# A fused time-attention, band-attention and feed-forward kernel: runs of eight steps, transposed copies on ACT, output products behind the scores, residual sums a run ahead

## The chip, the cores and the metric

The kernel runs on one core of one Trainium2 chip. The metric is device time in microseconds (us) of one execution. The kernel before took 3129.98 us, the median of 3 runs (3129.38 to 3130.77). Its profiled execution took 3130.63 us.

Names of the engines are those of the profile: PE (matrix products, with PEld for its weight loads), DVE (vector), ACT (scalar functions), POOL (GpSimd), SP (which issues the DMAs).

## The reference, cut to what matters

The input `x` has the shape 2 x 256 x 128 x 128 (batch, time T, band FB, channel C), all in float32. Three layers with residual sums follow one another; each head has 32 channels and there are 4 heads.

```python
xt = _ln(x, ...).transpose(0, 2, 1, 3)
x = x + _mha(xt, t_wi, t_bi, t_wo, t_bo, H_T, cm).transpose(0, 2, 1, 3)   # over time, causal mask
xf = _ln(x, ...)
x = x + _mha(xf, f_wi, f_bi, f_wo, f_bo, H_F, bm)                        # over bands, |i - j| <= 16
xn = _ln(x, ...)
h = jax.nn.gelu(xn @ w1.T + b1, approximate=False)                       # 128 -> 512 -> 128
x = x + (h @ w2.T + b2)
```

`_ln` subtracts the mean over the channels and multiplies with the inverse root of the variance. `_mha` is the usual attention: products for queries, keys and values, scores, softmax, weighted values, output product.

## The kernel before, in words

A short start-up folds the norms' weights into the product weights and tests whether the scores are bounded. They are for these inputs, so the program takes `bounded_path`, where softmax needs no maximum. (`shifted_path` is the other branch and does not run.)

The work is cut into **groups** of 512 tokens. There are three kinds, all classes with the same method names:

- `OverTime`: 128 groups, each two bands times 256 time steps. All of them come first, and write their result to DRAM (`x1`).
- `OverBands`: 128 groups, each 4 time steps times 128 bands, read from `x1`; they leave their result in SBUF, in a tile `x2` of 16 time steps.
- `FeedForward`: 128 groups, each on a quarter of an `x2` tile; they write the output.

In the second half of the program four `OverBands` groups and the four `FeedForward` groups on the same tokens take turns: 32 **cycles** of 4 + 4. Because gelu on one side and exponential and logarithm on the other are in different function tables of ACT, ACT loads a table at each turn.

The methods of a group, with the tiles by which the trace names them, are these. `load` starts the DMA of `xt` or `xb`. `statistics` makes mean and variance (`stats`, `mv`, on DVE) and in the same method the inverse root (`rstd`, on POOL). `normalize` makes `xh` (DVE, four instructions). `transpose` makes `xp` (PE, four transposes), and `take_transposed` copies it to SBUF as `xnT` (DVE). `queries_keys` and `values` are the products `qp`, `kp`, `vp`; they are copied to `qT` (ACT), `kT` (DVE for time groups, ACT for band groups) and `v` (ACT). The scores `sp` are products over 32 channels of one head, so four heads lie beside one another in four strips of 32 rows of PE. ACT takes the exponential (`pt` or `pf`), and POOL then cuts the mask out with selects; of the four heads of a band group, POOL does three with two selects each, and DVE the last by a product with a 0/1 tile `band`. `weigh` makes the row sums `rp` and the weighted values `op`; their weights are 32 columns wide, so four heads lie in four strips of columns. `invert` takes `ln` and `exp(-ln)` of the row sums on ACT (`ln`, `r`), and `divide` makes `oT` from it with three DVE instructions (`t`, `u`, `oT`). `divide_alone` does it with a DVE reciprocal instead, at one place per cycle. `output` is the output product `yp`, and `finish` adds it to the residual sum (`rd` or `x`), which `bias` prepared on POOL. A feed-forward group has four products `hp` with gelu (`hT`), sixteen small products `zp`, and its residual sum `res`.

The time groups split scores and exponential into two halves (`first_half`, `second_half`), feed-forward groups do so with their products; a band group does all in the first half.

The order of the work is written out by hand, by `run`: one pass of its loop is one **step** n. In a step, parts of several groups are interleaved: scores and exponential of group n, weighted values and division of group n - 1, the output product of group n - 2, the products for queries, keys and values of group n + 1, the transposes of group n + 2, the statistics of group n + 3. Each engine is wrapped in `InOrder`, which pins its instructions to the order of emission; all those instructions therefore carry one line number in the profile (L798, and L812 in the changed kernel). So an engine never passes a waiting instruction. DMAs are issued by SP, in order as well.

All PSUM tiles come from one pool of 8 banks, taken in turn. `xpool` has 3 buffers for `xt`/`xb` and, with a tag of its own, 2 for `x2`. The pool `work` has 3 buffers of most tiles, 2 of `t`, `u`, `oT`, `ln`, `r`, and 5 of `rd`.

Of the kernel before, what the change touches and what calls it, by code (L numbers as in the profile page):

```python
# [26 lines left out]
GB = 16  # L27
SAFE = 30.0
# [395 lines left out]
class Group:  # L424
# [4 lines left out]

    AHEAD = 2  # L430

# [12 lines left out]
    def statistics(self):  # L444
        path, vector, gpsimd = self.path, self.path.vector, self.path.gpsimd
        self.mv = path.small.tile([P, NT, 2], F32, name="mv")
        stats = path.small.tile([P, NT, 6], F32, name="stats")
        for i in range(NT):
            vector.bn_stats(stats[:, i, :], self.src()[:, i, :])
        for i in range(NT):  # L450
            vector.bn_aggr(self.mv[:, i, :], stats[:, i, :])
        self.rstd = path.small.tile([P, NT], F32, name="rstd")
        gpsimd.tensor_scalar(self.rstd, self.mv[:, :, 1], EPS, None, ALU.add)
        gpsimd.tensor_tensor(self.rstd, self.rstd, path.k.mhalf, ALU.pow)

    def normalize(self):
        path, vector = self.path, self.path.vector
        self.xh = path.work.tile([P, NT, P], F32, name="xh")
# [23 lines left out]

    def second_half(self):
        pass

    def second_function(self):
        pass
# [32 lines left out]
class Attention(Group):  # L520
# [60 lines left out]
    def divide_alone(self):  # L581

        path, vector = self.path, self.path.vector
        r = path.work.tile([P, NT * P], F32, name="r", bufs=2)
        vector.reciprocal(r, self.rp)
        self.oT = path.work.tile([P, NT * P], F32, name="oT", bufs=2)
        vector.scalar_tensor_tensor(self.oT, self.op, -1.0, r, ALU.mult, ALU.mult)

# [18 lines left out]
class OverTime(Attention):  # L607
# [26 lines left out]
    def weights(self, s):  # L634
        path = self.path
        for h in range(H):
            path.scalar.activation(self.p[:, s, h, :], self.sp[h], AF.Exp)
        for n in (0, 2):
# [12 lines left out]

    def second_half(self):
        self.scores(1)

    def second_function(self):
        self.weights(1)

# [23 lines left out]
class OverBands(Attention):  # L681


    which = 1

# [9 lines left out]
    def weights(self, heads):  # L695
        path = self.path
        for h in heads:
            path.scalar.activation(self.p[:, h].rearrange("p i q -> p (i q)"), self.sp[h], AF.Exp)
        for h in heads:
            blk = self.p[:, h]  # L700
            if h == H - 1:
                path.vector.tensor_tensor(blk, blk, path.band.unsqueeze(1).to_broadcast([P, NT, P]), ALU.mult)
                continue
            for s in (1, -1):
                path.gpsimd.affine_select(
                    out=blk, in_=blk, compare_op=ALU.is_ge, fill=path.zero, base=BAND,
                    pattern=[[0, NT], [-s, P]], channel_multiplier=s,
                )

# [8 lines left out]

    def first_function(self):
        self.weights(range(H))  # L720
# [17 lines left out]
class FeedForward(Group):  # L738
    AHEAD = 1
# [63 lines left out]
class BoundedPath:  # L803
# [22 lines left out]
    def groups(self, x, out):  # L826
# [28 lines left out]
        for b in range(B):  # L855
            x1v = k.x1[b].rearrange("t f c -> f t c")
            outv = out[b].rearrange("t f c -> f t c")
            for t0 in range(0, T, GB):
                held = {}

                def load(t0=t0, x1v=x1v, held=held):
                    held["x"] = self.xpool.tile([P, GB, C], F32, name="xb", tag="x")
                    nc.sync.dma_start(held["x"], x1v[:, t0 : t0 + GB, :])
                    held["x2"] = self.xpool.tile([P, GB, C], F32, name="x2", tag="x2", bufs=2)

                def part(name, g, held=held):
                    return lambda: held[name][:, g : g + NT, :]

                for g in range(0, GB, NT):
                    yield OverBands(self, part("x", g), part("x2", g), load if g == 0 else None)  # L870
                for g in range(0, GB, NT):

                    def store(t, g=t0 + g, outv=outv):
                        nc.sync.dma_start(outv[:, g : g + NT, :], t)

                    yield FeedForward(self, part("x2", g), None, None, store)

    def run(self, x, out):
# [7 lines left out]
        def near(n, far, name):  # L886

            for d in (1, 2):
                if 0 <= n + d + far < len(groups) and groups[n + d + far].AHEAD == d:
                    do(n + d + far, name)  # L890

# [3 lines left out]
        def move(n):  # L895
            near(n, 0, "transpose")
            near(n, 0, "take_transposed")

        self.scalar.preload_act_table_set(EXP_SET)
        for n in range(-7, len(groups) + 2):  # L900
            feeding = [at(n - i, FeedForward) for i in range(3)]
            do(n + 7, "load")
            near(n, 0, "normalize")
            if feeding[0] and at(n - 1, OverBands):

                do(n, "first_half", "first_function", "second_half", "second_function")
                do(n - 2, "output", "finish")
                near(n, 1, "statistics")
                move(n)
                do(n, "bias")  # L910
                do(n - 1, "weigh", "divide_alone")
            elif feeding[1] and at(n - 2, OverBands):
                do(n, "first_half", "first_function", "bias")
                do(n - 1, "weigh", "divide")
                move(n)
                do(n - 2, "output", "finish")
                near(n, 1, "statistics")
                do(n, "second_half", "second_function")
            else:
                do(n - 2, "output", "finish")  # L920
                near(n, 1, "statistics")
                if feeding[1] and at(n, OverBands):
                    self.scalar.preload_act_table_set(EXP_SET)
                do(n, "first_half", "first_function", "bias")
                early = at(n, OverBands) and at(n + 1, FeedForward)
                if early:
                    move(n)
                do(n - 1, "weigh", "invert", "divide")
                if feeding[0] and at(n + 1, FeedForward):
                    move(n)  # L930
                    early = True
                do(n, "second_half", "second_function")
                do(n + 1, "queries_keys", "take_query", "take_key", "values", "take_values")
                if not early:
                    move(n)
# [69 lines left out]
```

## Time and profile before

| what | value |
|---|---|
| median of 3 runs | 3129.98 us |
| time of the profiled execution | 3130.63 us |
| its span, first to last instruction | 3128.7 us |
| PE busy (matrix products) | 3013.3 us, 96% |
| PEld busy (weight loads) | 2133.5 us, 68% |
| DVE busy | 2246.7 us, 72% |
| ACT busy | 1748.6 us, 56% |
| POOL busy | 1889.3 us, 60% |
| granted clock of PE | 0.999 |
| ACT table loads | 64 of 1283 ns |
| POOL selects on `pf` | 768 of 711 ns |

The time of the profiled execution is 1.9 us above its span; the work stands in the span. A busy share is a mean over the whole program. In a row of the timeline the first number is the start, the second the time from the first start to the last end of the instructions that the row merges. Ends of products on PE are modelled and the next product usually starts ahead of them, so the price of a product on PE is read from its start to the next start. What stands in brackets is idle time of the engine ahead of that row, and what ended it.

### The profile page before, as it was taken

To read this page: it belongs to the slowest core of one execution; us is meant where nothing else is said; L and a number is where in the kernel's file an instruction comes from. 1 tells how busy PE (TensorE), PEld (TensorE's weight loads), DVE (VectorE), ACT (ScalarE), POOL (GpSimd) and SP (SyncE) were. 2 spreads that over 40 slices of the span, in tenths; PEclk is the share of its full clock that TensorE was granted. 3 is DMA by queue.
4 is the path that set the end of the run, shared out by engine and by line. 5 is a ranking of instruction groups with operands and counts; after the bars stand their busy time and mean duration, and the time that the engine had idled before them with its cause. 6 is when DMAs were issued, how large, how long until landed. Compare 5 with 4: busy or idle time off the path is not lost.

```text
span 3128.7 us, 77496 instructions
## 1 busy us (share of the span) xinstructions
PE 3013.3 (96%) x31270; PEld 2133.5 (68%) x31270; DVE 2246.7 (72%) x6414; ACT 1748.6 (56%) x3200; POOL 1889.3 (60%) x2441
## 2 busy tenths in 40 slices
PE   7999999999999999999999999999999999999998
PEld 5666666666666666666666666666666666776676
DVE  6776767777677677677767767776777677767775
ACT  4666666666666664554455445544554555455544
POOL 4666666666666665566556656665665566556654
PEclk9999999999999999999999999999999999999999
DMA  3222222222222221101111111111101110111000
GB/s 84 59 59 72 59 59 60 71 59 61 72 61 59 59 62 35 35 28 43 34 35 28 45 35 32 28 45 35 32 28 45 35 32 28 45 35 32 28 22 22
DMA packets 222863, 140.55 MB, mean 45 GB/s; under 512 B 7968, under 2 KB 205984, under 8 KB 222496
## 3 DMA queue, kind: packets, MB, share of 16 engines
q1 hardware_dynamic: 221248, 134.45, 15.3%
q8 instruction: 249, 4.08, 0.5%
q10 hardware_dynamic: 1248, 1.05, 0.1%
q14 instruction: 118, 0.97, 0.1%
HBM read 68.36 MB, written 67.11 MB: 43 GB/s over the span
## 4 chain that ended last, share of the span: by engine, by line
PE 80%; DVE 13%; ACT 5%; issue 1%; DMA 0%; POOL 0%; SPq 0%; ACTq 0%; POOLq 0%; DVEq 0%
PE zp L798 15%; PE hp L798 15%; PE sp L798 10%; PE yp L798 7%; PE rp L798 7%; PE qp L798 6%; PE op L798 6%; PE vp L798 5%; PE kp L798 5%; PE xp L798 4%; DVE xh L798 3%; ACT pf L798 3%; DVE stats L798 2%; DVE oT L798 2%; DVE t L798 1%; DVE x L798 1%
## 5 line engine op out<-in xcount | busy, mean ns | idle before, releaser
L798 POOL TENSOR_SCALAR rstd<-mv 128x4 f32<-128x4 f32 x384 | 99.2, 258 | 1131.9 <-DVE mv L798 1131.9
L798 ACT ACTIVATE hT<-hp,b 128x512 f32<-128x512 f32 x512 | 351.9, 687 | 620.8 <-PE hp L798 616.4
L798 ACT ACTIVATE pt<-sp 128x384 f32<-128x384 f32 x1024 | 419.3, 496 | 303.6 <-PE sp L798 303.6
L798 POOL TENSOR_SCALAR_AFFINE_SELECT pf<-pf 128x512 f32<-128x512 f32 x768 | 533.9, 711 | 38.6 <-ACT pf L798 12.3
L798 PEld LDWEIGHTS zp<-w2T_sb,hT 128*128 128x128 f32 x4096 | 475.0, 192 | 50.4 <-issue 38.7
L798 PE MATMUL hp<-xnT,w1f 128*128 128x512 f32 x1024 | 471.5, 598 | 34.0 <-DVE xnT L798 34.0
L798 PE MATMUL zp<-w2T_sb,hT 128*128 128x128 f32 x4096 | 481.5, 276 | 0.1
L798 DVE COPY xnT<-xp 128x512 f32<-128x512 f32 x384 | 260.0, 684 | 278.9 <-PE xp L798 278.9
L798 POOL TENSOR_TENSOR rstd<-rstd,mhalf 128x4 f32<-128x4 f32 x384 | 399.7, 1041 | 32.0
L798 PE MATMUL sp<-qT,kT 32*128 32x128 f32 (+1 forms) x8192 | 389.4, 315 | 0.0
L798 ACT ACTIVATE pf<-sp 128x512 f32<-128x512 f32 x512 | 264.4, 602 | 202.9 <-PE sp L798 202.6
L798 PEld LDWEIGHTS sp<-qT,kT 32*128 32x128 f32 x8192 | 310.8, 185 | 64.6 <-issue 35.9
L798 PEld LDWEIGHTS vp<-wf,xnT 128*128 128x128 f32 x2048 | 269.1, 192 | 123.0 <-issue 85.5
L798 PEld LDWEIGHTS hp<-xnT,w1f 128*128 128x128 f32 x1024 | 181.9, 190 | 218.6 <-issue 162.4
L798 PE MATMUL yp<-wn,oT 128*128 128x128 f32 x2048 | 275.1, 277 | 46.8 <-DVE oT L798 46.8
L798 POOL TENSOR_SCALAR_AFFINE_SELECT pt<-pt 128x512 f32<-128x512 f32 x512 | 314.4, 636 | 0.0
L798 PEld LDWEIGHTS yp<-wn,oT 128*128 128x128 f32 x2048 | 251.1, 192 | 73.9 <-ACT v L798 58.6
L798 PE MATMUL qp<-xnT,wf 128*128 128x512 f32 x512 | 282.7, 634 | 1.2 <-DVE xnT L798 1.2
L798 DVE TENSOR_TENSOR t<-rp,r 128x512 f32<-128x512 f32 x224 | 154.5, 690 | 174.8 <-ACT r L798 173.9
L798 PE MATMUL vp<-wf,xnT 128*128 128x128 f32 x2048 | 269.9, 275 | 0.0
L798 DVE TENSOR_SCALAR xh<-x,mv,rstd 128x128 f32<-128x128 f32 x512 | 256.3, 562 | 15.1 <-POOL rstd L798 15.1
L798 PE MATMUL kp<-xnT,wf 128*128 128x512 f32 x512 | 262.3, 594 | 0.0
(94 smaller groups left out, 4630.5 us busy)
## 6 DMA issues: line engine op xcount, KB each, us to landing
xt<-in_x SPq DMA_DIRECT2D x64, 512.0 KB, 5.5
x<-rd SPq DMA_DIRECT2D x256, 128.0 KB, 1.9
out<-res SPq DMA_DIRECT2D x128, 256.0 KB, 2.3
xb<-x SPq DMA_DIRECT2D x32, 0.5 KB, 6.1
w1T_sb<-in_w1T ACTq DMA_DIRECT2D x1, 256.0 KB, 3.8
w2T_sb<-in_w2T ACTq DMA_DIRECT2D x1, 256.0 KB, 4.2
t_wiT_sb<-in_t_wiT ACTq DMA_DIRECT2D x1, 192.0 KB, 2.5
f_wiT_sb<-in_f_wiT ACTq DMA_DIRECT2D x1, 192.0 KB, 3.9
```

The source lines that it names most:

```text
L798: return self.tc.keep_in_program_order(emit(*args, **kwargs))
```

## The change

What it does:

- **Longer runs.** Band groups and feed-forward groups now take turns in runs of 8 + 8 (`RUN = 32` time steps), 16 runs in place of 32 cycles. There are 4 `x2` buffers in place of 2, and 4 of `xh` in place of 3. Loads are issued 10 steps ahead, not 7.
- **Transposed copies.** `xnT` of band and feed-forward groups is copied by ACT, not DVE. Time groups keep DVE.
- **Output product behind the scores.** In a step, the scores of group n now come first, then the output product of group n - 2. Before it was the other way round.
- **Residual sums a run ahead.** `bias` of a band group (POOL) is made 8 steps ahead: in the feed-forward steps of the run before, or in the last eight time steps.
- **Split methods.** The inverse root leaves `statistics` and becomes `root`, which comes after `normalize`; masks leave the exponential's methods and become `first_mask` and `second_mask`. In the last band group of a run, DVE masks two heads and POOL two.
- **The turn.** All groups are now normalized two steps ahead (feed-forward groups before: one). `divide_alone` with its reciprocal is gone; in the first feed-forward step of a run, the last band group's `invert` stands between the two halves of gelu.

The diff, cut to its core:

```diff
+RUN = 32
...
     def statistics(self):
...
+
+    def root(self):
+        path, gpsimd = self.path, self.path.gpsimd
         self.rstd = path.small.tile([P, NT], F32, name="rstd")
         gpsimd.tensor_scalar(self.rstd, self.mv[:, :, 1], EPS, None, ALU.add)
         gpsimd.tensor_tensor(self.rstd, self.rstd, path.k.mhalf, ALU.pow)
...
-        path.vector.tensor_copy(self.xnT, self.xp)
+        if isinstance(self, OverTime):
+            path.vector.tensor_copy(self.xnT, self.xp)
+        else:
+            path.scalar.copy(self.xnT, self.xp)
...
-    def divide_alone(self):
...
+    def second_mask(self):
+        path = self.path
+        for h in range(H - self.by_vector, H):
+            blk = self.p[:, h]
+            path.vector.tensor_tensor(blk, blk, path.band.unsqueeze(1).to_broadcast([P, NT, P]), ALU.mult)
...
+            for r0 in range(0, T, RUN):
+                run = []
+                for t0 in range(r0, r0 + RUN, GB):
...
+                        held["x2"] = self.xpool.tile([P, GB, C], F32, name="x2", tag="x2", bufs=2 * RUN // GB)
...
+                    if i == len(run) - 1:
+                        g.by_vector = 2
...
-        for n in range(-7, len(groups) + 2):
-            feeding = [at(n - i, FeedForward) for i in range(3)]
-            do(n + 7, "load")
-            near(n, 0, "normalize")
-            if feeding[0] and at(n - 1, OverBands):
-
-                do(n, "first_half", "first_function", "second_half", "second_function")
-                do(n - 2, "output", "finish")
-                near(n, 1, "statistics")
-                move(n)
-                do(n, "bias")
-                do(n - 1, "weigh", "divide_alone")
...
+        for n in range(-10, len(groups) + 2):
+            feeds = [at(n - 2 + i, FeedForward) for i in range(5)]
+            bands = [at(n - 2 + i, OverBands) for i in range(5)]
+            do(n + 10, "load")
+            do(n + 3, "statistics")
+            if bands[2] and feeds[1]:
+                self.scalar.preload_act_table_set(EXP_SET)
+            do(n, "first_half", "first_function", "first_mask")
+            if feeds[1]:
+                if bands[0]:
+                    do(n - 2, "output", "finish")
                 do(n - 1, "weigh", "divide")
+            elif feeds[2]:
+                do(n - 1, "weigh", "invert", "divide")
+            else:
+                do(n - 2, "output", "finish")
+            if feeds[3]:
+                do(n + 1, "transpose", "take_transposed")
+            do(n + 2, "normalize")
+            do(n + 3, "root")
+            if not bands[2]:
+                do(n, "bias")
+                if at(n + RUN // NT, OverBands):
+                    do(n + RUN // NT, "bias")
+            if bands[2]:
+                do(n, "second_mask")
+            if not feeds[1] and not feeds[2]:
                 do(n - 1, "weigh", "invert", "divide")
+            do(n, "second_half", "second_function")
+            if not bands[2]:
+                do(n, "second_mask")
+            if feeds[2] and bands[1]:
+                do(n - 2, "output", "finish")
+            do(n + 1, "queries_keys", "take_query", "take_key", "values", "take_values")
+            if at(n + 2, Attention):
+                do(n + 2, "transpose", "take_transposed")
```

PE in the time stage, one step, before (`yp` belongs to group n - 2, the first two `sp` rows to group n):

```order
L798 MATMUL yp<-wn_106,oT 128x128 x4
L798 MATMUL sp<-qT,kT 128x256 x4
L798 MATMUL sp<-qT,kT 128x128 x4
L798 MATMUL rp<-pt,ones 32x512 x4
L798 MATMUL rp<-pt,ones 32x2x128 x4
L798 MATMUL op<-pt,v 32x256 x4
L798 MATMUL op<-pt,v 32x128 x4
```

And the same place now:

```order
L812 MATMUL sp<-qT,kT 128x256 x4
L812 MATMUL sp<-qT,kT 128x128 x4
L812 MATMUL yp<-wn_106,oT 128x128 x4
L812 MATMUL rp<-pt,ones 32x512 x4
L812 MATMUL rp<-pt,ones 32x2x128 x4
L812 MATMUL op<-pt,v 32x256 x4
L812 MATMUL op<-pt,v 32x128 x4
```

The full-size product `yp` stood ahead of the products in strips; now it stands between the strips of rows (`sp`) and the strips of columns (`rp`, `op`). In band steps the same two pieces change places.

DVE in the band stage, before, from the sum `x` of one step to that of the next (`x_15240` is a tile of residual sums):

```order
L798 TENSOR_TENSOR x_15240<-yp,x_15240 128x512
L798 BN_STATS stats<-x_15240 128x6 x4
L798 BN_AGGR mv<-stats 128x2 x4
L798 TENSOR_TENSOR pf<-pf,band 128x512
L798 TENSOR_TENSOR t<-rp,r_16398 128x512
L798 TENSOR_TENSOR u<-op,r_16398 128x512
L798 SCALAR_TENSOR_TENSOR oT<-t,u 128x512
L798 TENSOR_SCALAR xh<-x_15240,mv,rstd 128x128 x4
L798 TENSOR_TENSOR x_15240<-yp,x_15240 128x512
```

And now:

```order
L812 TENSOR_TENSOR x_14871<-yp,x_14871 128x512
L812 TENSOR_SCALAR xh<-xb,mv,rstd 128x128 x4
L812 TENSOR_TENSOR pf<-pf,band 128x512
L812 TENSOR_TENSOR t<-rp,r_16421 128x512
L812 TENSOR_TENSOR u<-op,r_16421 128x512
L812 SCALAR_TENSOR_TENSOR oT<-t,u 128x512
L812 BN_STATS stats<-xb 128x6 x4
L812 BN_AGGR mv<-stats 128x2 x4
L812 TENSOR_TENSOR x_14871<-yp,x_14871 128x512
```

The normalization `xh` has moved to between the sum `x`, which waits for `yp`, and the `oT` that the next `yp` waits for; the statistics have moved out of there.

ACT at the turn from the last band group of a run to feed-forward, before:

```order
L798 ACTIVATE pf<-sp 128x512 x4
L798 ACTIVATE ln<-rp 128x512
L798 ACTIVATE r_17865<-ln 128x512
L798 ACT_TABLE_LOAD
L798 ACTIVATE hT<-hp,b_181 128x512 x16
```

And now:

```order
L812 ACTIVATE pf<-sp 128x512 x4
L812 COPY xnT<-xp 128x512
L812 ACTIVATE ln<-rp 128x512
L812 ACTIVATE r_19705<-ln 128x512
L812 ACT_TABLE_LOAD
L812 ACTIVATE hT<-hp,b_181 128x512 x2
L812 ACT_TABLE_LOAD
L812 ACTIVATE ln<-rp 128x512
L812 ACT_TABLE_LOAD
L812 ACTIVATE r_19754<-ln 128x512
L812 COPY xnT<-xp 128x512
L812 ACT_TABLE_LOAD
```

Where one table load stood, four stand now (the last is followed by the other gelus), since `ln` and `r` of the last band group have come between the gelus. The program has 80 table loads on this path in place of 64.

More of the change, by code (lines that the diff above doesn't have):

```diff
@@ L457, in normalize @@
         path, vector = self.path, self.path.vector
-        self.xh = path.work.tile([P, NT, P], F32, name="xh")
+        self.xh = path.work.tile([P, NT, P], F32, name="xh", bufs=4)
         for i in range(NT):
@@ L481, in first_function, with first_mask @@
         pass
+    def first_mask(self):
+        pass
     def second_half(self):
@@ L486, in second_function @@
     def second_function(self):
+        pass
+    def second_mask(self):
         pass
@@ L693, in scores, with first_function, first_mask @@
                 path.tensor.matmul(self.sp[h][:, c], self.kT[r, c], self.qT[r, c], start=True, stop=True)
-    def weights(self, heads):
+    def first_function(self):
+        for h in range(H):
+            self.path.scalar.activation(self.p[:, h].rearrange("p i q -> p (i q)"), self.sp[h], AF.Exp)
+    def first_mask(self):
         path = self.path
-        for h in heads:
-            path.scalar.activation(self.p[:, h].rearrange("p i q -> p (i q)"), self.sp[h], AF.Exp)
-        for h in heads:
+        for h in range(H - self.by_vector):
             blk = self.p[:, h]
-            if h == H - 1:
-                path.vector.tensor_tensor(blk, blk, path.band.unsqueeze(1).to_broadcast([P, NT, P]), ALU.mult)
-                continue
             for s in (1, -1):
```

72 lines of the change are left out of this document (22 added, 50 removed).

## The prediction

> **What bounds the kernel now.** I first cut the program into its two stages with the table of windows. Behind each window stand its length and the busy time of PE, PEld, DVE, ACT and POOL.
>
> ```profile
> 60.00:1110.00 1050.00, 1050.00 (x12732) 723.25 (x12724) 739.32 (x2197) 678.88 (x1466) 660.08 (x857) 1.00 0.23 64
> 1150.00:3100.00 1950.00, 1860.16 (x17559) 1336.84 (x17552) 1433.23 (x3977) 1017.50 (x1632) 1177.33 (x1509) 1.00 0.12 34
> ```
>
> In the stage over time PE is busy for 1050.00 of 1050.00 us. There is no wait to remove; only a change in what PE does can move that stage. In the stage of bands and feed-forward PE lacks 89.8 us, so something can be won there. The waits of PE name it:
>
> ```profile
> PE yp L798 <- DVE oT L798: 46.8, 64, 0.9
> PE hp L798 <- DVE xnT L798: 34.0, 64, 0.8
> ```
>
> Both come 64 times, twice in each of the 32 cycles of four band and four feed-forward groups. PE waits for DVE: for the division `oT`, and at the turn to feed-forward for the transposed copy `xnT`. The timeline of PE over part of one cycle gives the prices, always from one start to the next:
>
> ```profile
> 2010.48 1.17 PE L798 MATMUL sp<-qT,kT 32*128 32x128 f32 x32
> 2011.58 1.06 PE L798 MATMUL rp<-pf,ones 128*32 128x512 f32 x8
> 2012.46 1.06 PE L798 MATMUL op<-pf,v 128*32 128x128 f32 x32
> 2013.45 1.13 PE L798 MATMUL qp<-xnT,wf 128*128 128x512 f32 x2
> 2014.41 1.02 PE L798 MATMUL kp<-xnT,wf 128*128 128x512 f32 x2
> 2015.27 1.05 PE L798 MATMUL vp<-wf,xnT 128*128 128x128 f32 x8
> 2016.16 0.60 PE L798 MATMUL xp<-ident,xh 128*128 128x128 f32 x4
> 2017.42 1.13 PE L798 MATMUL yp<-wn,oT 128*128 128x128 f32 x8 [0.66 <-DVE oT L798]
> 2018.47 1.17 PE L798 MATMUL sp<-qT,kT 32*128 32x128 f32 x32
> ...
> 2023.27 1.05 PE L798 MATMUL vp<-wf,xnT 128*128 128x128 f32 x8
> 2025.12 1.13 PE L798 MATMUL yp<-wn,oT 128*128 128x128 f32 x8 [0.80 <-DVE oT L798]
> ...
> 2027.29 0.55 PE L798 MATMUL xp<-ident,xh 128*128 128x128 f32 x3
> ...
> 2028.40 1.06 PE L798 MATMUL rp<-pf,ones 128*32 128x512 f32 x8
> 2029.28 1.06 PE L798 MATMUL op<-pf,v 128*32 128x128 f32 x32
> 2031.10 3.70 PE L798 MATMUL hp<-xnT,w1f 128*128 128x512 f32 x8 [0.76 <-DVE xnT L798]
> ...
> 2035.53 0.60 PE L798 MATMUL xp<-ident,xh 128*128 128x128 f32 x4
> 2036.06 1.09 PE L798 MATMUL rp<-pf,ones 128*32 128x512 f32 x8
> 2036.94 1.09 PE L798 MATMUL op<-pf,v 128*32 128x128 f32 x32
> 2038.33 1.95 PE L798 MATMUL hp<-xnT,w1f 128*128 128x512 f32 x4 [0.30 <-DVE xnT L798]
> ...
> 2043.69 0.60 PE L798 MATMUL xp<-ident,xh 128*128 128x128 f32 x4
> 2044.13 1.06 PE L798 MATMUL yp<-wn,oT 128*128 128x128 f32 x8
> 2045.02 3.60 PE L798 MATMUL hp<-xnT,w1f 128*128 128x512 f32 x8
> ```
>
> Two things are to be seen. First, products in strips (`sp`, `rp`, `op`) make their full-size neighbours dearer. `xp` costs 0.44 us ahead of `yp`, but 0.53 ahead of `rp`; `qp` costs 0.96 behind `op`, but `kp`, of the same shape, 0.86. So one visit of PE to the strips costs about 0.09 + 0.10 = 0.19 us. Second, the true loss at a wait is more than the bracket says. It is 1.26 - 0.44 = 0.82 at the first `yp`, 1.85 - 0.89 = 0.96 at the second (0.89 is `vp` from 2015.27 on), 1.11 - 0.63 = 0.48 at the `xp` that stands between strips (0.44 + 0.19), 1.82 - 0.99 = 0.83 at the first `hp` (0.99 is `op` from 2012.46 on) and 1.39 - 0.99 = 0.40 at the second. Together 3.49 us per cycle, 111.7 us in 32 cycles.
>
> **The change part by part.**
>
> *Waits that go.* The copy `xnT` leaves DVE, the feed-forward norm is made a step earlier, the reciprocal is gone, and `yp` moves behind `sp`, which gives `oT` 1.10 us more. If all five waits go, that is -111.7 us. Half as many turns alone would have taken about half.
>
> *Output product behind the scores.* In a time step PE ran `yp sp rp op sp` and now runs `sp yp rp op sp`: two visits to the strips, not one. PE is full there, so nothing hides the added 0.19 us: 127 steps make +24.1 us. In the band stage I counted the visits in the order of the products: 6 per cycle before, so 12 per eight groups of each kind, and 15 per run now; 3 x 16 x 0.19 = +9.1 us. Together +33 us. This part costs; bounds are 0 (if a weight load hides behind the strips after all) and twice 0.10 per visit, 35 us.
>
> *DVE in a band step.* A band step on PE without a wait now costs `sp` 1.10, `yp` 0.89 + 0.19, `rp` 0.88, `op` 0.99, `qp` 0.96, `kp` 0.86, `vp` 0.89, `xp` 0.53: 7.29 us. Against it stands a loop through DVE's queue: `oT`, then `yp` on PE, then its sum `x`, then `xh`, the band product on `pf`, `t`, `u` and the next `oT`. Rows of the full timeline:
>
> ```profile
> 2013.82 1.12 DVE L798 TENSOR_TENSOR pf<-pf,band 128x512 f32<-128x512 f32 x1 [0.64 <-ACT pf L798]
> ...
> 2018.65 0.69 DVE L798 TENSOR_TENSOR x<-yp,x 128x512 f32<-128x512 f32 x1 [0.78 <-PE yp L798]
> ...
> 2021.81 0.69 DVE L798 TENSOR_TENSOR pf<-pf,band 128x512 f32<-128x512 f32 x1 [1.28 <-ACT pf L798]
> 2021.94 4.82 POOL L798 TENSOR_SCALAR_AFFINE_SELECT pf<-pf 128x512 f32<-128x512 f32 x6
> ...
> 2022.96 0.69 DVE L798 TENSOR_TENSOR t<-rp,r 128x512 f32<-128x512 f32 x1 [0.46 <-ACT r L798]
> ...
> 2023.57 0.68 DVE L798 TENSOR_TENSOR u<-op,r 128x512 f32<-128x512 f32 x1
> 2024.29 0.69 DVE L798 SCALAR_TENSOR_TENSOR oT<-t,u 128x512 f32<-128x512 f32 x1
> ...
> 2024.90 3.19 DVE L798 TENSOR_SCALAR xh<-x,mv,rstd 128x128 f32<-128x128 f32 x4
> ...
> 2032.88 2.54 DVE L798 TENSOR_SCALAR xh<-x,mv,rstd 128x128 f32<-128x128 f32 x4
> ```
>
> From `oT` to `yp` 0.83 (2024.29 to 2025.12), from `yp` to `x` 1.23 (2017.42 to 2018.65), `x` 0.72, `t` 0.61, `u` 0.72: 4.11 us, and `xh` and `pf` besides. Both run while POOL cuts the masks, and both are slower then: `xh` takes 2.54 to 3.19, `pf` 0.69 to 1.12. That makes 7.34 to 8.42 us. I take 7.45: when the loop is the slower side, PE issues the scores, and so the masks, earlier against it, and the masks are over by the time of `pf`. The wait is then 0.15 us in six steps of a run, 0.9 us.
>
> *The turn to feed-forward.* ACT must pass more before the copy `xnT` of the second feed-forward group: three table loads, two gelus, `ln`, `r`, and the copy itself.
>
> ```profile
> 2002.83 1.28 ACT L798 ACT_TABLE_LOAD   x1
> 2004.13 2.06 ACT L798 ACTIVATE pf<-sp 128x512 f32<-128x512 f32 x4
> ...
> 2021.64 0.63 ACT L798 ACTIVATE ln<-rp 128x512 f32<-128x512 f32 x1
> ...
> 2032.26 0.69 ACT L798 ACTIVATE hT<-hp,b 128x512 f32<-128x512 f32 x1 [0.17 <-PE hp L798]
> ```
>
> With `r` taken as long as `ln` and the copy as long as a gelu, these are 3 x 1.28 + 3 x 0.69 + 2 x 0.63 = 7.2 us, counted from the `r` before, which is out some 2.4 us behind the start of its `rp` (1.07, a step of 0.1, and twice 0.63): 9.6 us. PE needs, from that `rp` to the `hp` of the second group, with an `hp` at the 0.86 of `kp`, 0.88 + 0.99 + 1.91 + 0.88 + 0.99 + 0.54 + 1.72 + 0.89 = 8.8 us. So PE waits there for about 0.8 us, once per run. Bounds are 0 and, if the copy also meets a late `rp`, 2 us.
>
> A table load is followed by the exponentials 0.02 us after its end, at 2004.13. The Trainium skill, page "ScalarE: Activation LUTs", section "What ACT_TABLE_LOAD costs", states about 1283 ns and a drain of about 1380 ns for each switch. By that the wait here would be 4.1 us more per run. This trace has the first number and no room for the second.
>
> *Answered in one way.* The residual sums made a run ahead take POOL (one more sum in each feed-forward step, one less in each band step) where PE waits for nobody now; they shift POOL's load out of the masks. ACT gains copies, but is busy for 1017.50 of 1950 us. Loads ten steps ahead and more buffers are off the path: a load may wait in SP's queue for a buffer with two steps' stores behind it, and five `rd` buffers cover that. I add 0.1 us per run for what these leave.
>
> **The sum.** Against the profiled execution: 3130.6 - 111.7 + 33.2 + 16 x (0.9 + 0.8 + 0.1) = 3081 us. The profiled execution lies 0.65 us above the median of the runs, which is nothing here. 0.2%, or 6 us, is about what a measurement can tell from no change.
>
> **The rivals.**
>
> *PE alone.* No wait is left: masks and norm do not meet, the turn is covered. 3130.6 - 111.7 + 33.2 = 3052 us. For it speaks that the loop's lower bound is only 0.05 over 7.29. Chance 0.18.
>
> *The DVE loop takes the place of the old wait.* In band steps `xh` and `pf` meet the masks in full: the loop takes 8.42, PE waits 1.13 in six steps, 6.8 us in place of 0.9 per run: 3081 + 94 = 3175 us, slower. It decides from the loop of 7.96 us on, where 6 x 0.67 us x 16 eat the rest of the gain. For it: both long rows stand above. Against it: the 3.19 has its longest part in another POOL instruction, the residual sum, which leaves the band steps. Chance 0.06 for slower, 0.07 for half of it (3105 to 3124), 0.02 for about no change.
>
> *The time stage waits.* The scores now follow the transposes directly, 0.99 us earlier, and need `kT` from DVE. If `kT` comes 0.5 us late, 127 steps cost 64 us: 3145. Against it: DVE is busy for 739 of 1050 us there. Chance 0.03.
>
> *A table switch costs more than its load.* With 1.38 us behind each of the three loads at the turn, 16 x 4.1 = 66 us are added: 3147 us, slower. The row at 2004.13 speaks against it. Chance 0.02. This is the rule of the page named above.
>
> **How the numbers follow.** My forecast has 0.62. With the first rival and the half case, faster by over 0.2% has 0.62 + 0.18 + 0.07 = 0.87; within 0.2% 0.02; slower 0.06 + 0.03 + 0.02 = 0.11. The range reaches down to PE alone and a little below, 3046, and up to 3118, a loop of about 7.84 us; beyond it lie the slower cases and the end of the half case.
>
> **What would show it.** In the changed profile a time step, from `rp` to `rp`, should have grown by 0.19 us, with PE full; were it unchanged, my price of the strips is wrong. Band steps should take 7.3 to 7.6 us from one `sp` to the next; 7.9 or more means that DVE's loop has taken over, and PE then waits at `yp` for `oT`. At the turn PE should wait once per run for `xnT` from ACT, 0.5 to 1 us. The forecast is wrong if a wait appears in feed-forward steps, where I expect none.

## The result and the profile after

The changed kernel takes 3059.27 us (median of 4 runs, 3058.57 to 3059.68). The kernel before took 3129.80 us on the same chip (median of 4). The ratio is 0.9774, 95% interval 0.9757 to 0.9791: faster by 70.5 us. The forecast was 3081 us, so the gain was larger than predicted. The profiled execution took 3059.68 us, its span is 3057.8 us, and the granted clock of PE was 0.999.

The busy times of the changed kernel:

```profile
PE 3027.1 (99%) x31270; PEld 2134.0 (70%) x31270; DVE 2090.3 (68%) x6206; ACT 1960.3 (64%) x3536; POOL 1787.2 (58%) x2409
```

The table of windows of the changed kernel (length, then the busy time of PE, PEld, DVE, ACT and POOL), first a window in the time stage, then one in bands and feed-forward:

```profile
60.00:1110.00 1050.00, 1050.00 (x12433) 710.74 (x12426) 844.27 (x2149) 676.96 (x1435) 595.10 (x840) 1.00 0.22 62
1170.00:3040.00 1870.00, 1863.00 (x17695) 1343.70 (x17694) 1162.45 (x3795) 1218.95 (x1973) 1126.60 (x1475) 1.00 0.12 35
```

In the second stage PE now lacks 7.0 us in 1870; before it lacked 89.8 in 1950. Behind the start-up, the list of the waits of PE in the changed kernel (total, how often, the longest) has one row:

```profile
PE hp L812 <- ACT xnT L812: 7.0, 16, 0.5
```

It comes once per run of eight. No row names `yp` and `oT` any more. Waits of less than 0.15 us are not in such a list.

**The time stage.** One step of PE in the kernel before, from `rp` to `rp`:

```profile
599.50 1.50 PE L798 MATMUL rp<-pt,ones 128*32 128x512 f32 x16
...
608.10 1.50 PE L798 MATMUL rp<-pt,ones 128*32 128x512 f32 x16
```

And in the kernel after:

```profile
603.20 1.50 PE L812 MATMUL rp<-pt,ones 128*32 128x512 f32 x16
...
609.50 0.60 PE L812 MATMUL xp<-ident,xh 128*128 128x128 f32 x4
610.03 0.94 PE L812 MATMUL sp<-qT,kT 32*128 32x256 f32 x16
610.90 1.16 PE L812 MATMUL yp<-wn,oT 128*128 128x128 f32 x8
611.98 1.50 PE L812 MATMUL rp<-pt,ones 128*32 128x512 f32 x16
```

The step has grown from 8.60 to 8.78 us. `yp` costs 1.08 from its start to the next, where it cost 0.98 in the kernel before (606.25 to 607.23 there). The `xp` ahead of strips costs 0.53, not the 0.44 that it cost ahead of `yp` (605.81 to 606.25). For comparison, `yp` costs 0.89 in the turn below, where it stands between full-size products.

**A band step.** PE from one group of scores to the next in the kernel after:

```profile
2132.40 1.17 PE L812 MATMUL sp<-qT,kT 32*128 32x128 f32 x32
2133.50 1.16 PE L812 MATMUL yp<-wn,oT 128*128 128x128 f32 x8
...
2139.70 1.18 PE L812 MATMUL sp<-qT,kT 32*128 32x128 f32 x32
```

It takes 7.30 us with no bracket: the 7.29 us that PE needs by itself. The same step on DVE:

```profile
2134.70 0.69 DVE L812 TENSOR_TENSOR x<-yp,x 128x512 f32<-128x512 f32 x1 [0.82 <-PE yp L812]
2135.30 2.31 DVE L812 TENSOR_SCALAR xh<-xb,mv,rstd 128x128 f32<-128x128 f32 x4
2137.53 0.68 DVE L812 TENSOR_TENSOR pf<-pf,band 128x512 f32<-128x512 f32 x1
2138.13 0.68 DVE L812 TENSOR_TENSOR t<-rp,r 128x512 f32<-128x512 f32 x1
2138.73 0.67 DVE L812 TENSOR_TENSOR u<-op,r 128x512 f32<-128x512 f32 x1
2139.44 0.69 DVE L812 SCALAR_TENSOR_TENSOR oT<-t,u 128x512 f32<-128x512 f32 x1
```

POOL beside it:

```profile
2134.32 4.39 POOL L812 TENSOR_SCALAR_AFFINE_SELECT pf<-pf 128x512 f32<-128x512 f32 x6 [1.60 <-ACT pf L812]
```

DVE waits 0.82 us for `yp` in each step, so it is DVE that is early. From a `yp` (2133.50) by its sum `x` to the next `oT` (2139.44) DVE takes 5.94 us; with 0.83 from `oT` to the `yp` that uses it (the distance in the kernel before, where PE did wait for it) the loop is 6.77 us. That is 0.53 below PE's 7.30. `xh` takes 2.23 us to the next start, although it lies within the six selects, and `pf` only 0.60; it starts at 2137.53, just ahead of the sixth select (2137.60).

The 0.53 holds for the four inner steps of a run. The step ahead of the last band group's scores takes 6.87 us, since no `xp` stands in it. There `oT` starts at 2035.57 and the `yp` that uses it at 2036.50, 0.93 later, which leaves only 0.10.

**The turn.** PE around the second feed-forward group of a run in the kernel after:

```profile
2045.89 1.05 PE L812 MATMUL yp<-wn,oT 128*128 128x128 f32 x8
2047.42 1.98 PE L812 MATMUL hp<-xnT,w1f 128*128 128x512 f32 x4 [0.48 <-ACT xnT L812]
2049.24 1.05 PE L812 MATMUL yp<-wn,oT 128*128 128x128 f32 x8
2050.13 3.74 PE L812 MATMUL zp<-w2T_sb,hT 128*128 128x128 f32 x32
```

And ACT there:

```profile
2043.06 1.28 ACT L812 ACT_TABLE_LOAD   x1
2044.35 0.60 ACT L812 ACTIVATE ln<-rp 128x512 f32<-128x512 f32 x1
2044.97 1.28 ACT L812 ACT_TABLE_LOAD   x1
2046.26 0.63 ACT L812 ACTIVATE r<-ln 128x512 f32<-128x512 f32 x1
2046.80 0.57 ACT L812 COPY xnT<-xp 128x512 f32<-128x512 f32 x1
```

The copy `xnT` ends at 2047.37, and `hp` starts 0.05 us later. From the first `yp` to `zp` PE takes 4.24 us here. Without a wait the same products take 3.50 us (the experiment with one table less shows them), so this turn costs 0.74 us. Four of the 16 turns take as long; the other twelve take 4.19 us.

### The profile page after: what moved, and what is told of

It reads as the page before. It is cut to its first block, busy times and chain, and to the rows that moved or that the text cites. A ratio compares the mean times of both kernels' runs of the same rounds, so it can differ in the third digit from the quotient of the medians.

```text
span 3057.8 us, 77275 instructions
## 1 busy us (share of the span) xinstructions
PE 3027.1 (99%) x31270; PEld 2134.0 (70%) x31270; DVE 2090.3 (68%) x6206; ACT 1960.3 (64%) x3536; POOL 1787.2 (58%) x2409
## 4 chain that ended last, share of the span: by engine, by line
PE 95%; DVE 3%; ACT 2%; DMA 0%; POOL 0%; issue 0%; SPq 0%; ACTq 0%; POOLq 0%; DVEq 0%
PE zp L812 15%; PE hp L812 13%; PE sp L812 12%; PE rp L812 9%; PE qp L812 9%; PE yp L812 8%; PE op L812 8%; PE vp L812 7%; PE kp L812 7%; PE xp L812 5%; DVE xh L812 1%; ACT L812 1%; DVE pf L812 0%; ACT r L812 0%; DVE stats L812 0%; ACT ln L812 0%
## 5 line engine op out<-in xcount | busy, mean ns | idle before, releaser
L812 POOL TENSOR_SCALAR_AFFINE_SELECT pf<-pf 128x512 f32<-128x512 f32 x736 | 499.0, 693 | 309.6 <-ACT pf L812 284.5
L812 DVE TENSOR_TENSOR res<-zp,res 128x512 f32<-128x512 f32 x128 | 88.6, 692 | 583.8 <-POOL x L812 330.7
L812 ACT ACTIVATE hT<-hp,b 128x512 f32<-128x512 f32 x512 | 344.8, 687 | 138.3 <-PE hp L812 135.9
L812 POOL TENSOR_TENSOR rstd<-rstd,mhalf 128x4 f32<-128x4 f32 x384 | 407.5, 1061 | 32.0
L812 ACT COPY xnT<-xp 128x512 f32<-128x512 f32 x256 | 150.5, 588 | 317.4 <-PE xp L812 317.4
L812 PE MATMUL yp<-wn,oT 128*128 128x128 f32 x2048 | 293.3, 286 | 0.0
L812 PE MATMUL xp<-ident,xh 128*128 128x128 f32 x1536 | 232.2, 274 | 10.1 <-DVE xh L812 10.1
```

Of the source, the lines that this page charges most:

```text
L812: return self.tc.keep_in_program_order(emit(*args, **kwargs))
```

## The experiments

All of them start from the changed kernel. The theory behind them: the old waits are gone because of the order of the work and the copies on ACT, PE is full, and three things still cost time that can be priced alone: the strips, the turn, and how near DVE's loop is to PE's step.

| kernel | median, us | ratio to the kernel before, 95% interval |
|---|---|---|
| the change | 3059.27 | 0.9774 (0.9757 to 0.9791) |
| output first in time steps | 3034.87 | 0.9696 (0.9680 to 0.9712) |
| output first everywhere | 3116.48 | 0.9956 (0.9939 to 0.9972) |
| copies on DVE | 3127.22 | 0.9990 (0.9980 to 0.9999) |
| one table less | 3047.80 | 0.9737 (0.9721 to 0.9753) |
| runs of four | 3073.71 | 0.9819 (0.9802 to 0.9835) |
| sums in their own step | 3071.54 | 0.9810 (0.9793 to 0.9826) |
| output behind the values | 3017.60 | 0.9638 (0.9622 to 0.9654) |
| the last and one table less | 3006.86 | 0.9605 (0.9589 to 0.9621) |
| division three times as long | 3169.21 | 1.0123 (1.0106 to 1.0140) |

### Output first in time steps only

```diff
+            early = not feeds[1] and not feeds[2] and not bands[2]
+            if early:
+                do(n - 2, "output", "finish")
             do(n, "first_half", "first_function", "first_mask")
...
-            else:
+            elif not early:
                 do(n - 2, "output", "finish")
```

> The changed kernel, but in the time steps the output product stands ahead of the scores again; band and feed-forward steps stay as changed. Theory (each extra visit of PE to the strips costs 0.19 us, and nothing in the time stage needed the move): 128 visits fewer, 3059 - 24.5 = 3035 us, a time step back at 8.59 us, no wait of PE there. Rival (the move bought the time stage something else, or the dearer product is only accounting): 3059 us, or a wait at the output product.

Measured: 3034.87 us, 24.4 less than the change. In the timeline of PE a time step takes 8.60 us again (from the second scores at 601.90 to those at 610.50), and the waits are those of the change. So the price of the strips in the time stage is shown: the move costs 24.4 us there (24.1 forecast) and buys nothing, since that stage has no wait to remove.

### Output first in band steps too

```diff
-            early = not feeds[1] and not feeds[2] and not bands[2]
+            early = not feeds[1] and not feeds[2]
```

> The changed kernel with the output product ahead of the scores in time and band steps. Theory: in a band step the loop then runs output product, scores, exponential, ln and r on ACT, t, u, oT, and next output product; by the rows of the changed kernel that is about 7.6 us, over the 7.1 us of PE alone, so PE waits for oT as in the kernel before. Band steps 7.6 in place of 7.3, six per run: 3035 + 29 = 3064 us. Rival (only the price of the strips counts, the division is early enough either way): 3059 - 24.5 - 16 = 3018 us, without a wait at the output product.

Measured: 3116.48 us, 81.6 more than with output first in time steps alone. PE waits again, 96 times for `oT`, once per band step in the inner part of a run:

```profile
PE yp L812 <- DVE oT L812: 62.0, 96, 1.0
```

PE, ACT and DVE in a band step of this kernel:

```profile
2135.91 1.13 PE L812 MATMUL yp<-wn,oT 128*128 128x128 f32 x8 [0.57 <-DVE oT L812]
2136.97 1.17 PE L812 MATMUL sp<-qT,kT 32*128 32x128 f32 x32
...
2138.22 2.06 ACT L812 ACTIVATE pf<-sp 128x512 f32<-128x512 f32 x4 [2.21 <-PE sp L812]
...
2140.14 0.63 ACT L812 ACTIVATE ln<-rp 128x512 f32<-128x512 f32 x1
...
2141.47 0.69 DVE L812 TENSOR_TENSOR t<-rp,r 128x512 f32<-128x512 f32 x1
...
2142.79 0.89 DVE L812 SCALAR_TENSOR_TENSOR oT<-t,u 128x512 f32<-128x512 f32 x1
...
2143.82 1.13 PE L812 MATMUL yp<-wn,oT 128*128 128x128 f32 x8 [0.57 <-DVE oT L812]
```

The step is 7.91 us, where PE by itself would need 7.29 - 0.19 = 7.10. With the output first, the scores wait behind it in PE's queue, the exponentials behind the scores, `ln` and `r` behind the exponentials in ACT's queue, and `t`, `u`, `oT` behind `r`. This loop closes on the next `yp`: from row to row 1.06 + 1.25 + 1.92 + 1.33 + 1.32 + 1.03 = 7.91 us. The theory was right in kind (waits at `yp` for `oT`), and its 7.6 us was too small; the rival, that the order does not matter here, fell. 0.61 us more than 7.30 in 96 steps would be 59 of the 82 us. The rest stands at the end of a run, where the change needs less than 7.30, and at the turn: from the first scores of one run to those of the next, this kernel takes 123.6 us on average and the change 118.4, and 16 times the difference is about the whole. In band steps the move behind the scores pays for its strips several times over.

### Transposed copies back on DVE

```diff
-        if isinstance(self, OverTime):
-            path.vector.tensor_copy(self.xnT, self.xp)
-        else:
-            path.scalar.copy(self.xnT, self.xp)
+        path.vector.tensor_copy(self.xnT, self.xp)
```

> The changed kernel with all transposed copies on DVE, as before. Theory: in band steps the copy fits between oT and the statistics, and costs nothing; at the turn it queues behind t, u, oT of the last band group, which wait for r on ACT, so the hp of the second feed-forward group comes about 2.3 us later: 16 x 2.3 = 37 us, 3096 us, all of it as a wait of hp for xnT from DVE. Rival A (DVE's queue is full in band steps, its loop grows by the copy): waits at the output product in each band step, 16 us or more on top. Rival B (the copies were hidden anyway): 3059 us.

Measured: 3127.22 us, 68 more than the change; nearly the whole gain is gone. The place is the one that the theory named, the turn, and not the inner band steps, which stay at 7.30 us. The size is more than twice the forecast one. PE at the turn in this kernel (the wait comes 16 times, 46.7 us in all by the list of waits):

```profile
2076.95 1.05 PE L809 MATMUL yp<-wn,oT 128*128 128x128 f32 x8
2080.99 3.20 PE L809 MATMUL hp<-xnT,w1f 128*128 128x512 f32 x4 [2.99 <-DVE xnT L809]
2083.99 1.53 PE L809 MATMUL yp<-wn,oT 128*128 128x128 f32 x8
2085.35 3.74 PE L809 MATMUL zp<-w2T_sb,hT 128*128 128x128 f32 x32
```

On DVE the copy stands behind `t`, `u` and `oT` of the last band group, and these behind the `r` that ACT makes after two more table loads. That is 3.15 us at `hp`. Then the products behind the wait are slow: four `hp` take 3.00 us where they took 1.82 in the change, and `yp` 1.36 in place of 0.89. The table of windows shows why; the first number behind the five engines is the mean granted clock:

```profile
2080.99:2085.35 4.36, 4.36 (x12) 2.58 (x13) 2.53 (x13) 1.37 (x2) 1.66 (x3) 0.61 0.02 4
```

It was 1.00 in the windows on both sides. From the first `yp` to `zp` the turn takes 8.40 us, 4.90 more than without a wait, and 4.16 more than in the change: 16 x 4.16 = 67 us, which is about the whole difference. The Trainium skill, page "TensorE: Matmul & The Clock Gate", Part 1, states that TensorE falls to half clock after an idle window of about 3.4 us. The trace agrees in kind; here an idle time of 2.99 us was enough.

### One table load less at the turn

```diff
             elif feeds[2]:
+                self.scalar.preload_act_table_set(EXP_SET)
                 do(n - 1, "weigh", "invert", "divide")
```

One table set holds both `ln` and the exponential, so the load between `ln` and `r` falls away (the profile counts 64 table loads in place of 80).

> The changed kernel with the table that holds both exp and ln requested ahead of the last band group's ln at the turn, so that ln and r share one load: 4 loads per run in place of 5. Theory (the wait of hp for xnT at the turn, 0.64 us in each of 16 runs, is the end of a chain on ACT with three loads of 1.28 us in it): one load less removes the wait, 3059 - 10 = 3049 us. Rival (a switch also costs a hidden drain of more than a microsecond, or ACT is not what the turn waits for): more than 10 us gained in the first case, nothing in the second.

Measured: 3047.80 us, 11.5 less than the change, as expected. The wait for `xnT` is gone from the list. PE at the turn in this kernel:

```profile
2040.85 1.05 PE L812 MATMUL yp<-wn,oT 128*128 128x128 f32 x8
2041.74 1.88 PE L812 MATMUL hp<-xnT,w1f 128*128 128x512 f32 x4
2043.46 1.05 PE L812 MATMUL yp<-wn,oT 128*128 128x128 f32 x8
2044.35 3.74 PE L812 MATMUL zp<-w2T_sb,hT 128*128 128x128 f32 x32
```

3.50 us in place of 4.24 or, in most turns, 4.19: 0.69 to 0.74 per turn, 11 to 12 us in 16. The bracket had named 0.48 of the 0.74. Another 0.16 lies ahead of `hp` too: `yp` takes 1.53 to the start of `hp` in the change and 0.89 here, but the bracket counts only from its modelled end. The other 0.10 is in `hp`, which takes 1.82 behind the wait and 1.72 without it.

### Runs of four

```diff
-RUN = 32
+RUN = 16
```

> The changed kernel with runs of four band and four feed-forward steps (RUN = 16, two x2 buffers), all else as changed. Theory (the gain came from waits that each turn had, not from having fewer turns): 16 turns more cost their 0.64 us wait each, 10 us, and 16 visits to the strips fewer give back 3 us: 3066 us, and the five waits of the old cycle do not return. Rival (the longer run is what hides the turn): about half of the old 112 us of waits returns, 3059 + 50 = 3110 us.

Measured: 3073.71 us, 14.4 more than the change. The waits of PE in this kernel:

```profile
PE hp L812 <- ACT xnT L812: 14.1, 32, 0.5
```

The turn comes 32 times and nothing else is listed: the rival, that the old waits come back with short runs, fell. From its first `yp` (2021.61) to `zp` (2026.00) the turn takes 4.39 us, so it costs 0.89 and not 0.74. Some of this is behind `hp`: the second `yp` starts at 2025.03, right behind its `oT` on DVE (2023.92 to 2024.89), which looks like one more wait, too short for the list. Of the difference, 32 x 0.89 - 16 x 0.74 = 16.6 us are turns; in the order of the products runs of four have 16 visits to the strips fewer, -3.0 us. That makes 13.6 of the 14.4. The theory had counted each turn at 0.64 us, the loss ahead of `hp` alone, and came out at half.

### Residual sums in their own step

```diff
-            if not bands[2]:
-                do(n, "bias")
-                if at(n + RUN // NT, OverBands):
-                    do(n + RUN // NT, "bias")
+            do(n, "bias")
```

> The changed kernel with each band group's residual sum made on POOL in its own step, behind the root, not a run ahead. Theory (POOL's step then is selects 4.4, root 1.3, sum 1.3: 7.0 of 7.3 us, and it ends before the next selects): no change, 3059 us within 5. Rival (the sum on POOL holds up the oT or the next selects, and through DVE's loop PE): some 0.3 us in six steps of a run, 3059 + 29 = 3088 us, as waits at the output product.

Measured: a median of 3071.54 us, but in two groups: four runs at 3070.1 to 3071.7 and two at 3095.5 and 3095.8. The profile is of the slower group, with a granted clock of 1.000. Its waits and, of DVE, two rows in one of its long band steps:

```profile
PE yp L812 <- DVE oT L812: 18.3, 44, 0.8
```

```profile
2138.96 2.74 DVE L812 TENSOR_SCALAR xh<-xb,mv,rstd 128x128 f32<-128x128 f32 x4
2141.62 1.13 DVE L812 TENSOR_TENSOR pf<-pf,band 128x512 f32<-128x512 f32 x1
```

With the sum POOL is hardly idle in a band step (it waits for `pf` 0 to 0.62 us here, 1.60 in the change), and its selects slide along DVE's `xh` and `pf`: here `xh` lasts 2.74 and `pf` 1.13 (in the change 2.31 and 0.68), and that step takes 8.00 us. The next one, with 2.20 and 0.68, takes 7.30. So the rival was right that the sums matter to DVE's loop, and the theory, that they lie off the path, fell. The listed wait of 18.3 us is about half of the 36 us between this profile and the change; in the 8.00 us step the scores themselves took 1.80 us in place of 1.10. Of their 32 products 26 start only at 2144.00, right behind the end of DVE's `u` at 2143.94, after a gap too short for the list. That PE waited there for DVE is likely, but not shown. What puts an execution into one group or the other, and what the 12 us of the faster group are, stays open.

### The output product behind other strips

```diff
-            else:
-                do(n - 2, "output", "finish")
...
-            if not feeds[1] and not feeds[2]:
-                do(n - 1, "weigh", "invert", "divide")
+            late = not feeds[1] and not feeds[2]
+            if late:
+                do(n - 1, "weigh")
+                if bands[2]:
+                    do(n - 2, "output", "finish")
+                do(n - 1, "invert", "divide")
             do(n, "second_half", "second_function")
+            if late and not bands[2]:
+                do(n - 2, "output", "finish")
```

`yp` then stands where the strips end and the full-size products begin: behind the second scores in a time step, behind `op` in a band step.

> The changed kernel with the output product behind the products in strips: behind the second scores in time steps, behind the weighted values in band steps (with its residual sum, in DVE's queue behind the band product). Theory (the 33 us for extra visits to the strips are a pure price, and a still later output product keeps the wait for oT away): 3059 - 24.5 - 16 = 3019 us, a time step 8.59, a band step 7.10 us, no wait at the output product. Rival (the sum x now stands directly ahead of t, u, oT in DVE's queue and waits for the output product, so t comes late and PE waits elsewhere): band steps of 7.3 us or more, 3035 us or more.

Measured: 3017.60 us, 41.7 less than the change, as expected. In the time stage of this kernel PE takes 8.60 us per step again, from `yp` (602.10) to `yp` (610.70). 24.4 of the gain are the time stage, as in the first experiment. The other 17.3 are band steps, where the order of the products has 5 visits to the strips fewer in each run: 5 x 16 x 0.19 = 15.2; the inner ones take 7.11 us. The loop through DVE does not come back: the scores stand ahead of `yp` here too.

### Both

> The kernel with the output product behind the values, and with one table load less at the turn as well. Theory (the two are independent: one is PE's own time, the other the end of ACT's chain): 3019 - 11 = 3008 us, with no wait of PE behind the start-up. Rival (with PE 0.2 us faster in each band step, another wait appears, for kT or for the weighted values' masks): 3019 us or more.

The two edits above together. Measured: 3006.86 us, as expected, 123 us below the kernel before and the best of these versions. Behind the start-up no wait of PE is left in the list.

### A division three times as long

```diff
-        vector.tensor_tensor(t, self.rp, self.r0, ALU.mult)
+        for _ in range(3 if self.which else 1):
+            vector.tensor_tensor(t, self.rp, self.r0, ALU.mult)
```

> Edit: in the changed kernel's band steps DVE computes t (the accumulator times the reciprocal) three times instead of once, between the first exps' values and oT; the output is the same. This lengthens DVE's loop from yp by oT back to yp by about 1.2 us (twice 0.60) and leaves every other engine's work alone; the time stage is untouched. It prices the term at which the forecast's sum was off: the slack of that loop in a band step of 7.30 us. Theory, the loop is 6.77 us as read from the profile (yp to oT 5.94 and oT to yp 0.83), 0.53 us of slack: the loop becomes 7.97, 0.67 us per band step are lost, 6 steps in each of 16 runs: +64 us, 3123 us, and TensorE waits at yp for oT about 96 times. Rival, the loop stands at 7.30 or above as the forecast had it (7.45) and only its waits are too short to be listed: the whole 1.2 us is lost, 96 times, +115 us, 3174 us. Second rival, DVE has far more slack than the chain shows since oT is used a step later than read: 3059 us and no wait.

Measured: 3169.21 us, 110 more than the change. By the time alone the first rival (the loop has no slack, 3174) seems right, and the theory (3123) wrong. The rows decide otherwise; the second rival, much more slack, falls with the time. The waits of PE come first. Then PE, at the `yp` of two inner band steps, of the last band group and of the turn; then DVE in an inner band step:

```profile
PE yp L813 <- DVE oT L813: 97.6, 107, 1.2
```

```profile
2183.06 1.13 PE L813 MATMUL yp<-wn,oT 128*128 128x128 f32 x8 [0.82 <-DVE oT L813]
...
2191.17 1.13 PE L813 MATMUL yp<-wn,oT 128*128 128x128 f32 x8 [0.77 <-DVE oT L813]
...
2215.53 1.13 PE L813 MATMUL yp<-wn,oT 128*128 128x128 f32 x8 [1.21 <-DVE oT L813]
...
2229.49 1.13 PE L813 MATMUL yp<-wn,oT 128*128 128x128 f32 x8 [1.13 <-DVE oT L813]
```

```profile
2187.58 2.13 DVE L813 TENSOR_TENSOR t<-rp,r 128x512 f32<-128x512 f32 x3
2189.62 0.68 DVE L813 TENSOR_TENSOR u<-op,r 128x512 f32<-128x512 f32 x1
```

The three `t` take 2.04 us from the first to `u`, so the edit adds 1.44 us, not the 1.2 that I had put in. The inner step grows from 7.30 to 8.11, by 0.81. So 0.63 of the 1.44 were slack, close to the 0.53 read from the change (`xh` lasts 2.20 here). The loss also comes 7 times per run, not 6: the output of the last group in the turn waits as well. From its first `yp` (2224.89) to `zp` (2230.45) that turn takes 5.56 us in place of 4.24, 1.32 more, and the `yp` of the last band group waits 1.21, for there the change had hardly any slack. Over a run it is 6.8 us more (125.3 in place of 118.4 from first scores to first scores), 109 us in 16. Slack of about 0.6 us in the inner steps is shown; my price of the edit and my count were off, I took the slack to be the same in all steps, and these errors added up near the rival's number by chance.

## Why the prediction was right or wrong

- **What bounds it, and the five waits (-111.7 us): right.** PE was the bound before and is so now. All five waits went, and stayed away in runs of four. So it is not the length of the runs that removed them; the longer run is worth 14.4 us. Two of the parts that did are shown by taking them back: the output product behind the scores in band steps (81.6 us) and the copies on ACT (68). The earlier norm and the dropped reciprocal were not taken back alone, so their share stays open.
- **The strips (+33.2 us): right.** 24.4 us of it are measured in the time stage by the first experiment. The band part was not measured by itself. The output product behind other strips takes 5 visits per run away there and gains 17.3 us, where 0.19 per visit makes 15.2. That this part of the change buys nothing in the time stage was in the forecast; what it does buy in band steps was in it only as 1.10 us more for `oT`. In truth it cuts the loop that runs from `yp` through the scores, ACT's queue and DVE back to `yp`, and that stood at 7.91 us without it.
- **DVE in a band step (0.9 us per run, 14.4 in all): wrong, and this is the step that failed.** I had the loop at 7.34 to 8.42 and took 7.45; it is 6.77 in the change, and no wait follows from it. Of the 0.68 between them, 0.17 is the fixed part: it is 0.83 + 1.20 + 0.60 + 0.60 + 0.71 = 3.94, not 4.11. Another 0.16 is a misreading: I took `xh` and `pf` by the length of their rows, but the next instruction of DVE starts about 0.08 ahead of each such end. The other 0.35 is the price of `xh` and `pf` beside POOL's masks. In the same measure, the length of the row, `xh` lasts 2.31, below the smaller of my ends (2.54, beside selects alone; the 3.19 stood beside the residual sum too), and `pf` 0.68, at my smaller end, since it gets in ahead of the sixth select; and I had added 0.11 to the smaller sum. The experiment on the sums shows the other side of this. With POOL nearly full, the same rows last 2.74 and 1.13 in some steps. I had seen that the loop and the masks shift against each other, but not carried it through. That PE sets the step and leaves DVE time cannot be the whole reason why the meeting is cheap: with the division three times as long DVE sets the step, and `xh` lasts 2.20 and `pf` 0.70 there. The dear cases of `xh` shown here stood beside the residual sum or a POOL almost without pause; a rule for the price is not shown.
- **The turn (0.8 us per run): right in place, cause and size.** It is 0.69 to 0.74.
- **The rest (0.1 us per run): nothing.** The residual sums are not without effect, as I had it under "answered in one way": made in their own step they cost 12 to 36 us. The change puts them where no wait is listed for them, so the sum was right, but not the reason.
- **The rival "PE alone"** comes nearest in time (3052): its lack of a wait in band steps holds, its covered turn does not. "The DVE loop takes the place of the old wait" fell in the change itself; the division three times as long and the output first show that the mechanism exists 0.6 us away. "The time stage waits" fell: PE is full there. "A table switch costs more than its load" fell: in the turn `ln` starts at 2044.35, where the load from 2043.06 ends, and the load taken away gave back 0.69 to 0.74 us per turn, all of the wait that there was. The 1.38 us of drain that the Trainium skill (page "ScalarE: Activation LUTs", section "What ACT_TABLE_LOAD costs") adds to each load is not seen here.

The sum with the measured terms, 0.74 taken for every turn, is 3130.6 - 111.7 + 33.2 + 16 x 0.74 = 3063.9 us against 3059.7 measured. 4.2 us, 0.26 per run, are not traced. From my 3081: 14.4 the loop, 1.6 the rest, 1.0 the turn, and these 4.2.

## What to carry to other kernels

Where two engines slow each other, the price of their meeting is no constant to be taken from the old schedule: `xh` lasted 3.19 and 2.54 before, 2.31 in the change and up to 2.74 with the sums in their own step. Work out how much slack the loop has without it, step by step, since a shorter step leaves less; and read a loop from start to start, not by the lengths of rows. An order in which a product stands ahead of work that it does not feed can close a loop through three engines' queues; moving it behind cuts the loop, and among places behind choose one that makes no further change between strips and full-size products. In a stage that has no wait, such a move only costs.

## What the runs showed of the hardware

- After a wait of 2.99 us PE's granted clock was 0.61 for the next 4.36 us, and the products there took up to 1.65 times as long (3.00 against 1.82 us). In the turn of the change, with a bracket of 0.48, it stayed at 1.00. A wait near 3 us thus costs more than its length: 4.90 us for 3.15.
- A short wait costs more than its bracket, too: in the turn of the change 0.74 for 0.48. 0.16 of the rest is how the bracket is counted, from a modelled end, and 0.10 is a dearer `hp` behind the wait, at full clock.
- Three products `t` in a row into one tile took 2.04 us to the next start on DVE, where a single one takes 0.60.
- With the sums in their own step, executions of one program fell in two groups 25 us apart, both at a granted clock of 1.00.
